# Pacing side work beside a first attention: scans given twice their share of a chain's order of work, and weight preparation that ends 2.4 batches in

## The chip, the cores and the metric

The kernel runs on one core of one Trainium2 chip. A core has a matrix engine (TensorE, PE in the profile; PEld is its weight load), a vector engine (VectorE, DVE), a scalar engine (ScalarE, ACT), a general engine (GpSimd, POOL) and SyncE (SP), which here issues all DMA transfers. The metric is device time in microseconds (us) of one execution; lower is better.

## The reference, cut to what matters

Eight batches of 64 rows of 512 values pass through six layers. The first is a large cross attention of 32 heads on a context of 1601 rows for each batch; the others are small by comparison.

```python
def reference(x, ctx_4096, ...):          # x (8, 64, 512), ctx_4096 (8, 1601, 512)
    x = x + xattn0(layernorm(x), ctx_4096)  # 32 heads of 128, 8 key/value heads, softmax, Wo
    x = x + mamba(layernorm(x))             # state space layer, below
    x = x + ternary_ffn(layernorm(x))       # 512 x 512 ternary weights, one scale
    x = x + xattn1(layernorm(x), ctx_4096)  # one head, softmax(x ctx^T) ctx, no weights
    x = x + attn1(layernorm(x))             # 32 heads of 16, rotary, causal
    x = x + oct_ffn(layernorm(x))           # gate, up, down; ternary, octonion structure
    return x

def mamba(h):                              # 1024 channels, 16 states
    x, gate = split(h @ W_in.T)
    x = silu(conv4(x) + conv_b)
    ts, Bm, Cm = rms each of split(x @ W_x.T)
    dt = softplus(ts @ W_dt.T + b_dt)
    for t in range(64):                    # the scan, for every channel and state
        state = state * exp(dt[t] * A) + dt[t] * x[t] * Bm[t]
        y[t] = sum over states of state * Cm[t]
    return ((y + x * D) * silu(gate)) @ W_out.T
```

Weights of the small layers are split into two float32r parts or made ternary before use. That preparation is part of the kernel: it reads the weights from HBM, works on them and writes the results to a scratch buffer in HBM.

## The kernel before, in words

**Main stream.** `x_all` is the first attention. It goes through 64 units, one for each batch and key/value head, 8 units to a batch. In each it projects keys (`x_k`, line 363) and values (`x_v`, line 334), multiplies scores (`x_s`, line 385), finds a row maximum (`mx`, lines 390 to 395), and one unit later takes exponentials (`x_exp`, lines 426 and 427), sums them on POOL (line 452) and multiplies by the values (`x_av`, line 464). After two batches it multiplies by Wo (`x_wo`, line 521) and adds into the tile `x1` (line 524). VectorE stands inside this loop: the copies of keys (`kt`, line 109), maxima and exponentials' inputs must be done before PE's next step can run, and the PSUM tag `kv` of those steps has 4 buffers.

**Side work.** Two kinds of generators run beside it. `prep` (lines 607 and on) prepares the weights: 100 steps of 1.5 to 3 units of cost, each of a load, one to three operations on ACT, DVE and POOL, and a store. In order these write `d_wout`, `d_ffn`, `d_wat`, `d_gu`, `d_dn` and `d_wo`. `chain` carries two batches through the five small layers. There are four chains, 0 to 3; one starts when its two batches have left the first attention. Chains 0 to 2 run beside the attention of later batches. Chain 3 starts when the attention has ended, in a different form (`tail`), with pools made anew in the memory that the attention and the first layers' tiles leave (`xctx.close()`, `actx.close()`).

**Order of work.** The order is written out by a small planner in `run`. Each yield of `x_all` gives a cost; their running sum divided by `X_COST = 236` is the position `now` in batches. A side generator has a total `cost`, a start and an end, and after each step of the main stream it is advanced until what it has yielded equals `cost * (now - start) / (end - start)`. So a yield's number is the share of the generator's window that the code before it gets. A chain's cost is `CHAIN_COST = 377`, and the lengths of its windows are `SPAN = [3.1, 3.1, 2.6, 0.2]` batches. Preparation has `PREP_COST = 168` and ends at `PREP_END = 2.8`. In units of cost, a side chain (0 to 2) yields, in order:

- `mamba`: convolution and its input 24, state inputs 3, `dt` 16, scans 128 (32 scans of 4 yields of 1, line 907 and on), gates and output 14.4
- `ternary_ffn` 9, `xattn1` 76 (38 for each batch), `attn1` 44, `oct_ffn` 33

The sum is 347.4, so a chain has yielded all before its window's end. When the attention ends, `now` goes on in steps of 0.01 with chain 3 first in the list and what is left of chain 2 behind it.

**Queues.** The Tile framework turns this program order into instruction queues by scheduling against a model of the machine, earlier work first. Side work on DVE, ACT and POOL is pinned: an instruction stays behind whatever was traced just before it on its engine (`Late`, line 65, which is why all of it stands under L65 in the profile). Instructions of the main stream are not pinned and may move ahead. PE and SP are not pinned. All chains and the preparation share 2 PSUM buffers of tag `acc`; the scans use none of them, but the `ca` pool's tags, `a2` with 5 buffers among them.

**One scan** (lines 893 to 916) is 4 of the 16 states of 128 channels: four exponentials on ACT, a memset and one or two products on POOL, yield, the scan on DVE, yield, a product with C on DVE or POOL in turn, yield, a reduction and an addition on DVE, yield. For each group of 8 scans two DMAs spread B and C over the partitions (line 889).

Of the kernel before, what the change touches and what calls it, by code (L numbers as in the profile page):

```python
# [78 lines left out]
class Kernel:  # L79
# [727 lines left out]
    def mamba(self, gi, x, xo):  # L807
# [87 lines left out]
        def scan(c, sh, bc):  # L895
            da = self.sb(self.td, [P, HS, 2, T])
            for s in range(HS):
                k = sh * HS + s
                nc.scalar.activation(da[:, s], dt[:, c], AF.Exp, scale=self.A[:, c, k : k + 1])
            nc.gpsimd.memset(da[:, :, :, 0:1], 0.0)  # L900
            du = dus[:, c]
            if sh == 0:
                nc.gpsimd.tensor_tensor(du, dt[:, c], u[:, c], ALU.mult)
            h = self.sb(self.ts, [P, HS, 2, T])
            nc.gpsimd.tensor_tensor(h, bc[:, 0], du[:, None].to_broadcast([P, HS, 2, T]), ALU.mult)

            yield 1
            hf, df = h.rearrange("p s b t -> p (s b t)"), da.rearrange("p s b t -> p (s b t)")
            nc.vector.tensor_tensor_scan(hf, df, hf, 0.0, ALU.mult, ALU.add)
            yield 1  # L910
            (nc.gpsimd if c % 2 else nc.vector).tensor_tensor(h, h, bc[:, 1], ALU.mult)
            yield 1
            y = da[:, 0]
            nc.vector.tensor_reduce(y.rearrange("p b t -> p (b t)"), h.rearrange("p s b t -> p (b t) s"), AX.X, ALU.add)
            nc.vector.scalar_tensor_tensor(u[:, c], u[:, c], self.Dp[:, c : c + 1] if sh == 0 else 1.0, y, ALU.mult, ALU.add)
            yield 1

        wps = None
        if tail:
# [43 lines left out]
        else:  # L963
            for sh in range(nh):
                bc = bcast(sh)
                for c in range(NCH):
                    yield from scan(c, sh, bc)
# [332 lines left out]
    def run(self):  # L1300
        nc, tc, ctx = self.nc, self.tc, self.ctx
        nc.scalar.preload_act_table_set("natural_log_exp_and_others")
        self.setup(bufs=BUFS, accb=2, hs=4, tail=False, ahead=1, **TAGS)
        self.pc = ctx.enter_context(tc.tile_pool(name="pc", bufs=2, space=PSUM))
        xctx = ctx.enter_context(ExitStack())
        self.px = xctx.enter_context(tc.tile_pool(name="px", bufs=2, space=PSUM))
        self.consts()
        self.scratch()
        self.xw = ctx.enter_context(tc.tile_pool(name="xw", bufs=2))
        self.xp = xctx.enter_context(tc.tile_pool(name="xp", bufs=2))  # L1310
        qctx = ctx.enter_context(ExitStack())
        self.q_ln(qctx.enter_context(tc.tile_pool(name="qp", bufs=2, side="right")))
        B = self.B
        sizes = GROUPS.get(B) or [1] * B
        groups, k = [], 0
        for m in sizes:
            groups.append(list(range(k, k + m)))
            k += m
        self.place = {b: (k * T, len(g) * T) for g in groups for k, b in enumerate(g)}
        side, self.tp = [], None  # L1320

        def start(gen, now, cost, end):
            env = {k: getattr(self, k) for k in ENV}
            if not self.tail:
                env["nc"] = Side(self, PINNED)
            side.append({"gen": gen, "cost": cost, "got": 0.0, "t0": now, "end": end, "env": env})

        def advance(now):
            base = {k: getattr(self, k, None) for k in ENV}
            for c in list(side):  # L1330
                self.setup(**c["env"])
                goal = c["cost"] * min(1.0, (now - c["t0"]) / max(c["end"] - c["t0"], 1e-9))
                if now >= c["end"]:
                    goal = 1e9
                while c["got"] < goal:
                    try:
                        c["got"] += next(c["gen"])
                    except StopIteration:
                        if PRINT_COST:
                            print("side", c["got"])  # L1340
                        side.remove(c)
                        break
            self.setup(**base)

        gi, now, xdone = 0, 0.0, 0.0
        for cost, fin in self.x_all(list(range(B))):
            xdone += cost
            if not self.flush:
                advance(xdone / X_COST)
            if fin == 0:  # L1350
                qctx.close()
                self.cp = ctx.enter_context(tc.tile_pool(name="cp", bufs=2, side="right"))
                actx = ctx.enter_context(ExitStack())
                self.ca = actx.enter_context(tc.tile_pool(name="ca", bufs=2, side="right"))
                start(self.prep(), xdone / X_COST, PREP_COST, PREP_END)
            if fin is not None and gi < len(groups) and groups[gi][-1] == fin:
                g = groups[gi]
                now = xdone / X_COST
                last = gi == len(groups) - 1
                if last:  # L1360
                    self.pinning = False
                    xctx.close()
                    actx.close()
                    self.pc = ctx.enter_context(tc.tile_pool(name="pt", bufs=3, space=PSUM))
                    self.ca = self.cp = self.tp = ctx.enter_context(tc.tile_pool(name="tp", bufs=2))
                    self.setup(bufs=BUFS_TAIL, accb=6, hs=8, tail=True, ahead=2, **TAGS_TAIL)
                start(self.chain(gi, g), now, CHAIN_COST, now + SPAN[gi])
                if last:
                    side.insert(0, side.pop())
                gi += 1  # L1370
        while side:
            now += 0.01
            advance(now)
# [4 lines left out]
ENV = ("nc", "cp", "ca", "pc", "bufs", "accb", "hs", "tail", "ahead", *TAGS)  # L1378
GROUPS = {8: [2, 2, 2, 2], 2: [2]}
SPAN = [3.1,3.1,2.6,0.2]  # L1380
PREP_END = 2.8
MAMBA_TAGS = ("a2", "lv", "bc", "xpad", "sm")
FFN_TAIL = (("l", 0), ("l", 1), ("a", 0), ("l", 2), ("a", 1), ("d", 0), ("a", 2), ("d", 1), ("d", 2))
REST = {"w2":8,"b4":3}
# [3 lines left out]
PREP_COST = 168.0  # L1388
PRINT_COST = False
CHAIN_COST = 377.0  # L1390


@with_exitstack
# [106 lines left out]
```

## Time and profile before

| | |
|---|---|
| runs | 2731.54 us median of 3 (2730.45 to 2734.26) |
| profiled execution: span, first to last instruction | 2719.3 us |
| its own time | not listed apart from its span; the median lies 12.2 us above the span |
| mean granted clock of TensorE | 0.977 |
| busy: PE, PEld, DVE, ACT, POOL | 94%, 84%, 64%, 50%, 43% |
| DMA | 455.59 MB, 52.2% of 16 engines' span |
| DVE scans of chains 0, 1, 2 (first to last start) | 769 to 1041, 1411 to 1691, 2033 to 2308 us |
| `mamba` ends in chains 0, 1, 2 (its `xr` starts being written) | 1124.2, 1784.6, 2387.8 us |
| last store of prepared weights is issued | 879.7 us |
| the attention's last result (`x1`, line 524) starts | 2423.2 us |
| chain 2's last result, chain 3's last result (line 1294) | 2702.3, 2715.6 us |

A busy share is the sum over stages that have different limits. In a table of stretches of time, each engine's busy time stands beside the length of the stretch, and PEclk is the share of full clock that the throttle granted TensorE there. Idle time of PE matters as long as PE is what the stretch is short of.

### The profile page before, as it was taken

The numbers are of one execution on the slowest core, as the hardware profiler recorded it, in microseconds if no ns is written. First come the engines' busy times: TensorE is split into PE (matmuls) and PEld (weight loads), VectorE is DVE, ScalarE is ACT, GpSimd is POOL, SyncE is SP. The second block draws the span as 40 slices with busy tenths as digits, with TensorE's granted clock in tenths as the row PEclk, the third lists the DMA queues.
The fourth block names the chain that finished last, engine by engine and source line by source line (L and its number), as shares of the span: only waits on it lengthen the run. The fifth ranks groups of instructions, "written<-read, shape, count | busy, mean of one in ns | idle before, by whom it ended". The sixth has DMA issues, their size and how long they took to land.

```text
span 2719.3 us, 43920 instructions
## 1 busy us (share of the span) xinstructions
PE 2565.7 (94%) x16288; PEld 2273.7 (84%) x16288; DVE 1746.8 (64%) x2843; ACT 1352.6 (50%) x3128; POOL 1171.4 (43%) x1123
## 2 busy tenths in 40 slices
PE   7999999999998899999999988999999998986888
PEld 6999999889887899978988987997897898964644
DVE  4544345577688886545568689544668879457854
ACT  4444554445565554544455554544555455445543
POOL 3212434464588643422357346421249445114610
PEclk9999999999999999999999998999999999997999
DMA  9544446665665234665234443565342463476575
GB/s 308 153 141 153 138 144 228 200 204 178 214 218 188 75 121 159 211 184 174 88 109 134 152 136 106 185 206 186 116 133 80 128 187 113 148 256 201 195 264 188
DMA packets 302934, 455.59 MB, mean 168 GB/s; under 512 B 80248, under 2 KB 179576, under 8 KB 298240
## 3 DMA queue, kind: packets, MB, share of 16 engines
q1 hardware_dynamic: 302720, 452.79, 52.2%
q8 instruction: 128, 2.10, 0.3%
q14 instruction: 86, 0.70, 0.1%
HBM read 380.23 MB, written 72.48 MB: 166 GB/s over the span
## 4 chain that ended last, share of the span: by engine, by line
PE 47%; DVE 11%; DMA 4%; POOL 3%; issue 3%; ACT 2%; POOLq 0%; DVEq 0%; ACTq 0%; SPq 0%
PE v_ps L334 10%; PE k_ps L363 10%; PE o_ps L464 6%; PE s_ps L385 5%; DVE a L65 4%; PE w_ps L521 2%; PE acc L819 2%; PE acc L777 2%; PE acc L774 1%; PE acc L1092 1%; PE acc L1036 1%; POOL a L65 1%; POOL ss L452 1%; DVE acc L953 1%; PE acc L1178 1%
## 5 line engine op out<-in xcount | busy, mean ns | idle before, releaser
L363 PE MATMUL k_ps<-cxb,wk 128*128 128x384 f32 x2304 | 473.5, 348 | 36.4 <-DVE kt L109 12.6
L334 PE MATMUL v_ps<-wv,cxb 128*128 128x256 f32 x3456 | 474.1, 283 | 7.4 <-DVE mx L392 3.9
L334 PEld LDWEIGHTS v_ps<-wv,cxb 128*128 128x128 f32 x3456 | 441.8, 190 | 28.9 <-issue 13.6
L363 PEld LDWEIGHTS k_ps<-cxb,wk 128*128 128x128 f32 x2304 | 406.8, 192 | 56.3 <-DVE kt L109 14.3
L385 PE MATMUL s_ps<-q,kt 128*128 128x256 f32 (+1 forms) x2496 | 414.5, 299 | 8.6 <-DVE mx L392 7.2
L464 PE MATMUL o_ps<-S,v 128*128 128x256 f32 (+1 forms) x1664 | 413.6, 381 | 2.6 <-DVE rw L479 1.7
L388 ACT COPY S<-s_ps 128x512 f32<-128x512 f32 (+1 forms) x448 | 242.5, 554 | 252.6 <-PE s_ps L385 249.0
L385 PEld LDWEIGHTS s_ps<-q,kt 128*128 128x128 f32 (+1 forms) x2496 | 342.0, 185 | 30.3 <-DVE mx L392 8.5
L392 DVE TENSOR_TENSOR mx<-s_ps,mx 128x512 f32<-128x512 f32 x256 | 175.4, 685 | 297.5 <-ACT S L388 297.2
L452 POOL TENSOR_TENSOR ss<-ss,S 128x512 f32<-128x512 f32 x254 | 356.6, 1404 | 14.9 <-ACT S L427 0.3
L429 POOL TENSOR_TENSOR ss<-S,S 128x512 f32<-128x512 f32 x64 | 84.0, 1312 | 640.0 <-ACT S L427 639.9
L464 PEld LDWEIGHTS o_ps<-S,v 128*128 128x128 f32 (+1 forms) x1664 | 299.4, 190 | 41.6 <-issue 5.6
L426 DVE TENSOR_TENSOR S<-S,m_ps 128x512 f32<-128x512 f32 (+1 forms) x448 | 257.5, 641 | 36.2 <-PE m_ps L412 35.4
L108 ACT ACTIVATE kt<-k_ps,c_bk 128x384 fp32r<-128x384 f32 (+1 forms) x256 | 151.8, 593 | 246.2 <-PE k_ps L363 245.4
L427 ACT ACTIVATE S<-S 128x512 f32<-128x512 f32 (+1 forms) x448 | 247.6, 600 | 41.4 <-DVE S L426 41.0
L109 DVE SCALAR_TENSOR_TENSOR kt<-k_ps,c_bk,kt 128x384 fp32r<-128x384 f32 (+1 forms) x256 | 160.9, 629 | 156.2 <-ACT kt L108 155.0
L337 ACT COPY v<-v_ps 128x256 f32<-128x256 f32 (+1 forms) x416 | 152.1, 368 | 195.8 <-PE v_ps L334 192.7
L334 PE MATMUL v_ps<-wv,cxt 128*128 128x256 f32 (+1 forms) x1536 | 211.3, 286 | 5.1 <-DVE mx L392 5.1
L334 PEld LDWEIGHTS v_ps<-wv,cxt 128*128 128x128 f32 (+1 forms) x1536 | 194.6, 176 | 17.3 <-issue 5.9
L363 PE MATMUL k_ps<-cxt,wk 128*128 128x450 f32 x768 | 179.3, 376 | 0.0
L65 DVE TENSOR_TENSOR_SCAN a<-a,a 128x512 f32<-128x512 f32 x96 | 153.9, 1603 | 32.2 <-POOL a L65 32.0
L65 ACT ACTIVATE a<-lv,c_A_log 128x128 f32<-128x128 f32 x384 | 122.8, 392 | 85.8 <-DVE a L65 84.8
(358 smaller groups left out, 3951.3 us busy)
## 6 DMA issues: line engine op xcount, KB each, us to landing
wo<-d_wo SPq DMA_DIRECT2D x96, 512.0 KB, 5.6
wk<-d_wk SPq DMA_DIRECT2D x63, 512.0 KB, 4.3
wv<-d_wv SPq DMA_DIRECT2D x31, 1024.0 KB, 5.7
cst<-in_ctxT_dram SPq DMA_DIRECT2D x96, 192.0 KB, 2.7
b<-in_ctxN_dram SPq DMA_DIRECT2D x36, 512.0 KB, 3.8
d_q<-q_t SPq DMA_DIRECT2D x32, 512.0 KB, 4.3
q<-d_q SPq DMA_DIRECT2D x64, 256.0 KB, 3.0
d_wo<-b SPq DMA_DIRECT2D x32, 512.0 KB, 2.9
```

The lines of the kernel that those rows point to most:

```text
L65: return lambda *a, **k: self.tc.keep_in_program_order(f(*a, **k))
L109: eng.scalar_tensor_tensor(lo, src, bias, hi.bitcast(FP), ALU.add, ALU.subtract)
L334: nc.tensor.matmul(ps[:r], lhsT=cx[:, a, c, o : o + r], rhs=w[:, m, c, :], start=k == 0, stop=k == 11)
L337: nc.scalar.copy(vt[:r], ps[:r])
L363: nc.tensor.matmul(ps[:, :wd], lhsT=w[:, a, c, :], rhs=cx[:, m, c, :], start=k == 0, stop=k == 11)
L385: nc.tensor.matmul(sp[:r, gi, :], lhsT=kt[:, a, o : o + r], rhs=q[:, m, :], start=k == 0, stop=k == 2)
L388: nc.scalar.copy(s[:r, :n], sp[:r, :n])
L392: nc.vector.tensor_tensor(mx, sp, S[0] if len(S) == 1 else mx, ALU.max)
L426: nc.vector.tensor_tensor(sv, sv, ps[:r, 1:2].to_broadcast([r, w, 256]), ALU.add)
L427: nc.scalar.activation(sv, sv, AF.Exp, scale=ISC)
L452: nc.gpsimd.tensor_tensor(ss, ss, S[n], ALU.add)
L464: nc.tensor.matmul(ps[:, 0], lhsT=self.v[(b, j, t)][:r, hc : hc + P], rhs=S[t // 2][:r, t % 2], start=t == 0, stop=t == NT - 1)
```

## The change

The four yields of a side chain's scan become 2 in place of 1, so that a chain's scans yield 256 units and not 128. The planner is told: a chain that is not the last has a cost of 377 + 128 = 505. Windows (`SPAN`) stay. So the scans get 256 of 505 parts of a window where they had 128 of 377, and every other step of a chain is spread over 377/505 = 0.747 of the positions that it had. The last chain is untouched. Preparation of weights, whose steps and cost stay, ends at 2.4 batches. No instruction is added or removed; what changes is the order in which the program is written, and what the scheduler makes of it.

```diff
--- before.py
+++ after.py
@@ -904,16 +904,16 @@
             h = self.sb(self.ts, [P, HS, 2, T])
             nc.gpsimd.tensor_tensor(h, bc[:, 0], du[:, None].to_broadcast([P, HS, 2, T]), ALU.mult)
 
-            yield 1
+            yield 2
             hf, df = h.rearrange("p s b t -> p (s b t)"), da.rearrange("p s b t -> p (s b t)")
             nc.vector.tensor_tensor_scan(hf, df, hf, 0.0, ALU.mult, ALU.add)
-            yield 1
+            yield 2
             (nc.gpsimd if c % 2 else nc.vector).tensor_tensor(h, h, bc[:, 1], ALU.mult)
-            yield 1
+            yield 2
             y = da[:, 0]
             nc.vector.tensor_reduce(y.rearrange("p b t -> p (b t)"), h.rearrange("p s b t -> p (b t) s"), AX.X, ALU.add)
             nc.vector.scalar_tensor_tensor(u[:, c], u[:, c], self.Dp[:, c : c + 1] if sh == 0 else 1.0, y, ALU.mult, ALU.add)
-            yield 1
+            yield 2
 
         wps = None
         if tail:
@@ -1364,7 +1364,7 @@
                     self.pc = ctx.enter_context(tc.tile_pool(name="pt", bufs=3, space=PSUM))
                     self.ca = self.cp = self.tp = ctx.enter_context(tc.tile_pool(name="tp", bufs=2))
                     self.setup(bufs=BUFS_TAIL, accb=6, hs=8, tail=True, ahead=2, **TAGS_TAIL)
-                start(self.chain(gi, g), now, CHAIN_COST, now + SPAN[gi])
+                start(self.chain(gi, g), now, CHAIN_COST if last else CHAIN_COST + SCAN_MORE, now + SPAN[gi])
                 if last:
                     side.insert(0, side.pop())
                 gi += 1
...
 SPAN = [3.1,3.1,2.6,0.2]
-PREP_END = 2.8
+PREP_END = 2.4
...
 CHAIN_COST = 377.0
+SCAN_MORE = 128.0
```

## The prediction

> **What bounds the kernel now.** I read the engines' shares first, then a table of stretches, then the groups of VectorE in the scans' stretches, the waits of PE there, and last the starts of each layer's last write.
>
> ```profile
> PE 2565.7 (94%) x16288; PEld 2273.7 (84%) x16288; DVE 1746.8 (64%) x2843; ACT 1352.6 (50%) x3128; POOL 1171.4 (43%) x1123
> ...
> PE   7999999999998899999999988999999998986888
> ...
> DVE  4544345577688886545568689544668879457854
> ```
>
> PE is nearly always busy and dips where DVE's digits reach 7 to 8: while scans run, and in the tail from 2412 us on. Stretches (us; then busy time of PE, PEld, DVE, ACT, POOL; granted clock; DMA share; GB/s):
>
> ```profile
> 640.00:768.00 128.00, 124.52 (x821) 115.95 (x820) 93.87 (x160) 70.41 (x160) 68.46 (x65) 0.97 0.62 201
> 768.00:855.00 87.00, 73.48 (x454) 69.37 (x453) 77.60 (x82) 48.45 (x116) 75.27 (x70) 0.92 0.66 218
> 855.00:1045.00 190.00, 180.09 (x1189) 171.63 (x1187) 157.51 (x218) 106.26 (x262) 118.27 (x114) 0.99 0.37 112
> 1045.00:1300.00 255.00, 254.85 (x1675) 222.02 (x1675) 131.30 (x246) 118.47 (x271) 70.14 (x68) 1.00 0.57 183
> 1411.00:1600.00 189.00, 185.37 (x1244) 170.94 (x1243) 144.72 (x214) 104.93 (x249) 110.27 (x107) 1.00 0.44 136
> 1600.00:1695.00 95.00, 78.41 (x453) 71.71 (x452) 85.71 (x112) 45.37 (x122) 49.22 (x52) 0.89 0.33 106
> 2033.00:2222.00 189.00, 180.32 (x1168) 160.87 (x1167) 154.59 (x217) 102.56 (x253) 120.57 (x118) 0.99 0.39 116
> 2222.00:2310.00 88.00, 80.78 (x503) 74.46 (x502) 75.83 (x111) 46.72 (x119) 48.52 (x48) 0.98 0.47 145
> 2412.00:2719.00 307.00, 241.20 (x1338) 154.24 (x1337) 193.04 (x366) 141.09 (x372) 89.55 (x96) 0.88 0.67 224
> ```
>
> Without scans (1045 to 1300) PE has no gap. With scans and `prep` together (768 to 855) it idles 13.5 of 87 us. Chain 1 shows what density does, by the scans' group on DVE from 1411 to 1600 and from 1600 to 1695:
>
> ```profile
> L65 DVE TENSOR_TENSOR_SCAN a<-a,a 128x512 f32<-128x512 f32 x15 | 24.0, 1601 | 3.3 <-POOL a L65 3.2
> L65 DVE TENSOR_TENSOR_SCAN a<-a,a 128x512 f32<-128x512 f32 x18 | 27.6, 1536 | 6.7 <-POOL a L65 6.7
> ```
>
> One scan in 12.6 us cost PE 3.6 us in 189; one in 5.3 us cost 16.6 us in 95. There PE waits for the main stream's own DVE work, queued behind scans:
>
> ```profile
> PE k_ps L363 <- DVE mx L392: 4.7, 1, 4.7
> PE s_ps L385 <- DVE mx L392: 4.5, 1, 4.5
> ```
>
> **Where the change puts things.** I turn planned positions into times by the unit then running in this trace (the transposes on line 412 open each). Scans of chains 0, 1, 2 are planned for 764 to 1054, 1346 to 1677, 1951 to 2224 us and began at 769, 1411, 2033. Their new plan is 735 to 1178, 1322 to 1795, 1922 to 2333: one in 13.8, 14.8 and 12.8 us, against 9.1, 10.3 and 8.5. Preparation's plan ends at 745, not 868 (its last store is issued at 880). The end of chain 2's `mamba` moves from 2252 to 2355.
>
> **Scans spread.** A scan step issues four exponentials on ACT (0.39 us each), a memset and products on POOL (1.3 to 1.4 us), the scan (1.54 to 2.47), a product on DVE or POOL (1.0 or 1.3), a reduction (1.06) and an addition (0.5): 3.6 us of DVE on average. All remains; 8 scans still share two DMAs through SP. What can go is PE's loss. Idle time while scans run is 13.5 + 9.9 = 23.4 us (chain 0), 3.6 + 16.6 = 20.2 (chain 1), 8.7 + 7.2 = 15.9 (chain 2). Lost clock is at most (1 - granted) x length: 8.9, 10.5 and 3.7 more. At the sparse rate, 3.6/15 = 0.24 us, 32 scans cost 7.7 us. So chain 0 gains 15.7 to 24.6; I take 19, between them, since POOL's preparation leaves as well. Chain 1 gains 12.5 to 23.0, nothing if the bunch only moves; I take 12.5, idle alone, since it starts late. Chain 2: if scans begin at 2033 again, 300 us are left to 2333, one in 9.4 us, which is nearest to 2033 to 2222 (189/19 = 9.9 us, 8.7/19 = 0.46 us each): 32 cost 14.7, a gain of 1; bounds are a loss of 6 (more of them bunched) and a gain of 11.9. Sum: 32.5.
>
> **Preparation earlier.** The same steps, with 2 DMAs each for the split ones, pass ACT, DVE, POOL and SP in 367 planned us rather than 490. What they cost PE without scans is 4.4 us idle from 378 to 640, 3.5 from 640 to 768 and 3.8 of clock: 11.7. In proportion to work nothing changes; with the square of density it grows by a third. I take +4, bounds 0 and +12. Main-stream transfers that share SP with its 32 stores of `d_wo` meet them some 120 us earlier; the first `wo` read that needs them belongs to batch 3, past 900, so no one waits for the result. What covered the late stores, the scans of chain 0, loses them.
>
> The scans' own time shows that neighbour: 2472 ns each from 768 to 855 beside `prep` on POOL, 1606 from 855 on. The Trainium skill, SBUF — State Buffer, section Who interferes with whom, states that a VectorE instruction with two SBUF inputs and a GpSimd instruction reading SBUF shut each other out for a whole instruction. That speaks against spreading: a sparse scan meets the attention's own POOL sums instead, and by 1601 against 1536 ns 96 scans would pay 6 us more of DVE time. No term here holds those 6 us.
>
> **The rest of a chain, denser.** 1045 to 1300 shows `mamba`'s output, `ternary_ffn` and `xattn1` with 0.15 us of PE idle and DVE at 51%. Packed into 0.747 of the positions, their DVE above the attention's own (44% from 120 to 378) rises by some 3 points, far from the 82% of 2033 to 2222. A stretch like 640 to 768 (2.7% idle) over the 341 + 353 planned us of chains 0 and 1 would cost 19. I take +3, bounds 0 and +19. Scans of the next chain now lie beside all of `attn1` and `oct_ffn`; the `dt` step no longer does. Today its second half waits for an `acc` buffer from 1307.8 to 1383.0 (line 872) behind `attn1`'s projections, 18 us each by weight loads (line 774).
>
> **The tail.** These DVE lines end chain 2's `mamba`, chain 2 and chain 3:
>
> ```profile
> 2387.77 0.69 DVE L65 TENSOR_TENSOR xr<-acc,x 128x512 f32<-128x512 f32 x1 [1.20 <-PE acc L777]
> ...
> 2702.34 0.75 DVE L1294 SCALAR_TENSOR_TENSOR xr<-acc,s_oct,xr 128x512 f32<-128x512 f32 x1
> ...
> 2715.59 0.75 DVE L1294 SCALAR_TENSOR_TENSOR xr<-acc,s_oct,xr 128x512 f32<-128x512 f32 x1 [2.92 <-PE acc L777]
> ```
>
> `mamba` ended 36, 78 and 136 us behind its plan in chains 0, 1, 2. From 2355 that is 2391 to 2491; I take 2415, between the first two since `dt` meets less, just before the attention's last sum at 2423. Chain 3 is then not held. Chain 2's rest took 2702.3 - 2387.8 = 314.5 us; from 2415 it ends at 2729.5, past today's 2719.3: +10. Bounds: +67 if `mamba` ends at 2491 and chain 3's memory waits for it; -16 if chain 3's 128 projections on line 819 (35 us for 19.1 of PE) run alone since chain 2 comes later.
>
> **Sum.** -32.5 + 4 + 3 + 10 = -15.5: span 2703.8. The median stands 12.2 above the span; with that unchanged, 2716.0 us.
>
> **Rivals.** Slower by the tail: chain 2's `mamba` ends after 2423 and holds chain 3 one for one. For it: the lateness grew along the chains. Against it: bunched scans cannot delay it once few are overdue, and the engines are free after 2412. It decides from 2423 + 25.5 = 2449 on; at 2465 it gives -25.5 + 42 = +16.5, 2748. Slower by density: chain 1 gains nothing, preparation costs 12 and the rest 19: -19 - 1 + 12 + 19 + 10 = +21, 2753. For it: PE idles 3.5 us from 640 to 768, where a chain's start meets `prep`. Against it: 1045 to 1300. No change: what sets the scans' pace is lateness, not the order (chains 1 and 2 began 65 and 82 us late), so only chain 0 beside `prep` gains 9 (13.5 to the 5% of 855 to 1045), against 4 + 3: about 2730.
>
> **How the numbers follow.** Likeliest 0.54, own range 2692 to 2726; tail 0.22; density 0.10; no change 0.14. A measurement tells 0.2%, 5.5 us, from no change. The best ends of all terms give -75, the worst +88, and need all terms at once; 2688 leaves out one in ten below, 2760 one above. Faster 0.54, same 0.14, slower 0.32.
>
> **What would show it.** Right: scans near 740 to 1180, 1400 to 1800 and 2030 to 2330 without a bunch like 1600 to 1695; no `d_wo` store after about 770; PE idle near 8 us in each of the first two chains' scans; chain 2's `mamba` ended before the attention's last sum, and its last result at the end of the trace. Wrong: scans still bunched at the end, or chain 3's first layer norm waiting for chain 2.

## The result, and the profile after

The changed kernel takes 2742.32 us (median of 9 runs, 2736.41 to 2747.24). Beside it the kernel before took 2731.54 us (9 runs, 2724.19 to 2735.69). The ratio is 1.0043, 95% interval 1.003 to 1.0055: slower by 0.3 to 0.55%. The prediction said 2716.0 us and faster. The time lies within the whole range that it gave, 2688 to 2760, but outside the 2692 to 2726 of its likeliest case, and the sign is wrong. The nearest forecast is that of its rival "slower by the tail", 2748.

A warning on the traces. In the profiled executions the span went from 2719.3 to 2741.3 us, 22.0 us more, but the medians are only 10.8 us apart. All later profiled executions took 1.7 to 2.5 us more than their span, so the profiled execution of before took about 2721 us, some 10 us below its median. The trace of preparation alone (first experiment) is a better base: it is the first step of the change, and its execution took 2733.22 us against a median of 2733.31. Two more profiled executions were short, that of {2} by 5.1 us and that of the kernel with a window of 2.3 by 7.1; the rest lie within 2.2 us of their medians.

The engines' shares and slices of the changed kernel:

```profile
PE 2570.2 (94%) x16288; PEld 2280.3 (83%) x16288; DVE 1703.3 (62%) x2843; ACT 1353.1 (49%) x3128; POOL 1174.0 (43%) x1123
...
PE   7999999999998999999999998899999999757887
...
DVE  4544345766768766656656658756576657848754
...
PEclk9999999999999999999999999999999999877998
```

The dip of PE in slice 13 stays, but the next slice is full. The dip of chain 1 is still there (slices 25 and 26), and a new one opens in slices 35 to 37, just where the attention ends.

Stretches of the changed kernel (us, length, busy PE, PEld, DVE, ACT, POOL, granted clock, DMA share, GB/s). The first row holds 25 of chain 0's 32 scans (the other 7 start by 1125, and PE has no idle time from 1045 to 1130), the second the work after them; then come chain 1's scans before and after chain 0's last result; then chain 2's scans before and after chain 1's last result; then the wait for chain 2, and the tail:

```profile
814.00:1045.00 231.00, 222.37 (x1467) 211.78 (x1466) 175.56 (x257) 127.39 (x310) 139.80 (x133) 0.99 0.34 102
1130.00:1354.00 224.00, 224.00 (x1519) 199.75 (x1518) 129.17 (x244) 109.54 (x253) 64.64 (x63) 1.00 0.48 152
1354.00:1650.00 296.00, 295.22 (x1912) 264.24 (x1911) 179.90 (x304) 149.74 (x347) 129.99 (x126) 1.00 0.47 148
1650.00:1762.00 112.00, 89.96 (x530) 82.73 (x529) 103.66 (x132) 61.31 (x160) 82.71 (x79) 0.91 0.44 131
1984.00:2306.00 322.00, 319.95 (x2065) 286.51 (x2064) 207.07 (x344) 167.43 (x388) 143.05 (x140) 1.00 0.46 147
2306.00:2378.00 72.00, 51.53 (x299) 46.14 (x297) 65.27 (x84) 31.71 (x90) 44.59 (x46) 0.84 0.20 63
2378.00:2438.00 60.00, 36.09 (x140) 25.70 (x140) 19.45 (x41) 12.81 (x33) 4.35 (x8) 0.76 0.44 140
2438.00:2741.00 303.00, 236.48 (x1332) 155.53 (x1332) 193.08 (x374) 140.21 (x374) 91.00 (x93) 0.86 0.69 229
```

Chain 0's scans now cost PE 8.6 us in 231. Chains 1 and 2 do as before, only more sharply: PE idles 0.8 us in 296 and then 22.0 in 112; 2.0 in 322 and then 20.5 in 72. DVE is busy 93% and 91% of the time in those two bunches. In them the scans' group on DVE reads (chain 1, then chain 2):

```profile
L65 DVE TENSOR_TENSOR_SCAN a<-a,a 128x512 f32<-128x512 f32 x18 | 31.4, 1746 | 3.6 <-POOL a L65 3.6
L65 DVE TENSOR_TENSOR_SCAN a<-a,a 128x512 f32<-128x512 f32 x14 | 22.6, 1618 | 5.0 <-POOL a L65 5.0
```

So 18 and 14 of the 32 scans run after the older chain's last result, one every 6.1 and 5.0 us. Doubling their share did not remove the bunches. In the kernel before it was 16 and 10, behind last results at 1608.9 and, 57.1 us earlier than now, at 2249.1:

```profile
2249.11 0.74 DVE L65 SCALAR_TENSOR_TENSOR xr<-acc,s_oct,xr 128x512 f32<-128x512 f32 x1
```

The end of the attention in the changed kernel, by VectorE's instructions in order of time (start, us, line, operation, tiles):

```profile
2306.19 0.73 DVE L65 SCALAR_TENSOR_TENSOR xr<-acc,s_oct,xr 128x512 f32<-128x512 f32 x1
...
2405.67 0.69 DVE L524 TENSOR_TENSOR x<-w_ps,x 128x512 f32<-128x512 f32 x1 [3.59 <-PE w_ps L521]
...
2437.49 0.69 DVE L65 TENSOR_TENSOR xr<-acc,x 128x512 f32<-128x512 f32 x1 [11.11 <-PE acc L777]
2438.10 0.68 DVE L141 BATCH_NORM_STATS2 ln_st<-x 128x6 f32<-128x512 f32 x1
...
2732.09 0.75 DVE L1294 SCALAR_TENSOR_TENSOR xr<-acc,s_oct,xr 128x512 f32<-128x512 f32 x1 [0.97 <-PE acc L777]
...
2737.22 0.75 DVE L1294 SCALAR_TENSOR_TENSOR xr<-acc,s_oct,xr 128x512 f32<-128x512 f32 x1 [2.92 <-PE acc L777]
```

These are, in order: chain 1's last result, the attention's last sum, the end of chain 2's `mamba`, chain 3's first layer norm, and the last results of chains 2 and 3. The attention ends 17.5 us earlier than before (2423.2), but chain 2's `mamba` ends 49.7 later (2387.8), and chain 3 starts directly behind it, 32.4 us after the attention's last sum. In the kernel before it started 1.2 us behind that sum:

```profile
2423.17 0.67 DVE L524 TENSOR_TENSOR x<-w_ps,x 128x512 f32<-128x512 f32 x1
...
2424.36 0.68 DVE L141 BATCH_NORM_STATS2 ln_st<-x 128x6 f32<-128x512 f32 x1
```

In every run of this study in which that `mamba` ended after the attention, chain 3 started 0.6 us behind it; in every run in which it ended before, chain 3 started 0.7 to 1.2 us behind the attention. The hold is shown. That its cause is the memory chain 3 shares with the first layers' tiles is read from the code and was not tried: chain 3's first layer norm also stands directly behind that `mamba`'s last instruction on VectorE, so the order of VectorE's own queue would show the same.

I split the span at chain 3's first layer norm: 2424.4 + 294.9 before, 2438.1 + 303.2 after. Below, "start" is the first part and "tail" the second. Against preparation alone, the better base (2424.2 + 307.2), the start is 13.9 us longer and the tail 4.0 shorter: the loss is the hold.

How much of the attention's 17.5 us was real? From 120 us to its end, first before, then after:

```profile
120.00:2423.00 2303.00, 2229.68 (x14415) 2033.00 (x14413) 1501.16 (x2403) 1159.04 (x2662) 1052.34 (x994) 0.99 0.50 157
```

```profile
120.00:2406.00 2286.00, 2214.66 (x14310) 2023.86 (x14308) 1449.01 (x2376) 1153.37 (x2643) 1053.01 (x993) 0.98 0.49 155
```

PE's idle time is 73.3 us before and 71.3 after. Of the 17 us, 2.0 are idle time saved and 15.0 are PE work: 105 matmuls, nearly all of chain 2, that used to run beside the attention and now run behind it.

### The profile page after: what moved, and what is told of

It reads as the page before. It is cut to its first block, busy times and chain, and to the rows that moved or that the text cites. A ratio compares the mean times of both kernels' runs of the same rounds, so it can differ in the third digit from the quotient of the medians.

```text
span 2741.3 us, 44008 instructions
## 1 busy us (share of the span) xinstructions
PE 2570.2 (94%) x16288; PEld 2280.3 (83%) x16288; DVE 1703.3 (62%) x2843; ACT 1353.1 (49%) x3128; POOL 1174.0 (43%) x1123
## 4 chain that ended last, share of the span: by engine, by line
PE 33%; DVE 9%; DMA 4%; POOL 2%; ACT 1%; issue 1%; SPq 0%; DVEq 0%; POOLq 0%
PE v_ps L334 6%; PE k_ps L363 6%; PE o_ps L464 4%; DVE a L65 4%; PE s_ps L385 3%; PE acc L774 2%; PE acc L777 2%; PE w_ps L521 1%; PE acc L819 1%; PE acc L1036 1%; PE acc L1178 1%; PE acc L1092 1%; POOL a L65 1%; PE acc L776 1%; DMA a<-in_W_inT_dram 1%
## 5 line engine op out<-in xcount | busy, mean ns | idle before, releaser
L363 PE MATMUL k_ps<-cxb,wk 128*128 128x384 f32 x2304 | 474.7, 348 | 29.0 <-DVE mx L392 11.7
L452 POOL TENSOR_TENSOR ss<-ss,S 128x512 f32<-128x512 f32 x254 | 354.6, 1396 | 15.7 <-ACT S L427 0.3
L65 DVE TENSOR_TENSOR_SCAN a<-a,a 128x512 f32<-128x512 f32 x96 | 147.4, 1536 | 30.4 <-POOL a L65 28.3
```

The lines of the kernel that those rows point to most:

```text
L65: return lambda *a, **k: self.tc.keep_in_program_order(f(*a, **k))
L363: nc.tensor.matmul(ps[:, :wd], lhsT=w[:, a, c, :], rhs=cx[:, m, c, :], start=k == 0, stop=k == 11)
L452: nc.gpsimd.tensor_tensor(ss, ss, S[n], ALU.add)
```

## The experiments

Each table column is read from the trace of that kernel: the end of the attention (its last sum starts), the end of chain 2's `mamba`, chain 3's start and the tail. "Left" is how many scans of chains 1 and 2 start after the older chain's last result. Ratios are against the kernel before on the same chip, with 95% intervals. Chains in braces are those with the doubled share.

| kernel | attention ends | `mamba` 2 ends | start + tail | left, 1 / 2 | median | ratio |
|---|---|---|---|---|---|---|
| before | 2423.2 | 2387.8 | 2424.4 + 294.9 | 16 / 10 | 2731.54 | 1 |
| preparation to 2.4 alone | 2423.0 | 2387.6 | 2424.2 + 307.2 | 16 / 10 | 2733.31 | 1.0026 [1.0016, 1.0036] |
| {0} | 2400.2 | 2404.8 | 2405.4 + 316.6 | 13 / 10 | 2724.75 | 0.9997 [0.9983, 1.001] |
| {1} | 2398.6 | 2399.9 | 2400.5 + 315.1 | 19 / 8 | 2717.28 | 0.9954 [0.9937, 0.9971] |
| {2} | 2424.8 | 2397.3 | 2425.5 + 293.7 | 16 / 16 | 2726.34 | 1.0003 [0.9992, 1.0014] |
| {0, 1} | 2398.0 | 2398.6 | 2399.2 + 313.8 | 18 / 8 | 2714.80 | 0.9960 [0.9945, 0.9975] |
| {0, 2} | 2397.3 | 2406.8 | 2407.4 + 301.1 | 13 / 16 | 2712.43 | 0.9945 [0.993, 0.9959] |
| {1, 2} | 2404.2 | 2419.3 | 2419.9 + 309.4 | 19 / 14 | 2729.78 | 0.9998 [0.9985, 1.0011] |
| {0, 1, 2}: the change | 2405.7 | 2437.5 | 2438.1 + 303.2 | 18 / 14 | 2742.32 | 1.0043 [1.003, 1.0055] |

All rows from the second on have preparation end at 2.4.

### The two halves of the change

Preparation alone, in the kernel before:

```diff
-PREP_END = 2.8
+PREP_END = 2.4
```

> Preparation ends at 2.4, scans keep their old share. Theory 'held tail' (the changed kernel is slower because chain 2's mamba ends after the attention and holds chain 3): this edit leaves chain 2's plan alone, so its mamba ends near 2388 us and before the attention's last sum, and only the gain of scans without preparation beside them is left: 2715 to 2727 us. Rival 'density' (denser side steps cost the attention PE time): preparation is denser by a third, 2733 to 2742 us.

Measured: 2733.31 us beside 2726.92, ratio 1.0026. The attention ended at 2423.0, 0.2 us from before, and its stretch shows the same idle time (74.4 us against 73.3):

```profile
120.00:2423.00 2303.00, 2228.64 (x14412) 2029.13 (x14410) 1481.91 (x2404) 1155.14 (x2662) 1053.98 (x995) 0.99 0.50 157
```

So inside the attention the move costs nothing and gains nothing. The held tail's 2715 to 2727 was missed. The 2733 to 2742 that the density theory expected was hit, but not by its mechanism. The 12 us that this trace has more than that of before all lie behind the attention, with the same 1284 matmuls there (the row of before is 2424 to 2719: 232.01 of 295.00 busy, clock 0.88):

```profile
2424.00:2731.00 307.00, 236.84 (x1284) 153.16 (x1284) 188.79 (x356) 138.00 (x366) 87.55 (x92) 0.84 0.64 215
```

They arise late, in chain 3 alone. Chain 2's last result starts at 2702.2 us (2702.3 before), chain 3's at 2727.7 (2715.6). The rows from 2424 to 2600 are alike (PE 132.2 us before, 131.2 here); those from 2640 to 2700, first before, then here, are not:

```profile
2640.00:2700.00 60.00, 53.00 (x266) 31.97 (x264) 28.01 (x51) 24.84 (x49) 8.27 (x9) 1.00 0.76 261
2640.00:2700.00 60.00, 47.24 (x220) 25.24 (x220) 25.58 (x50) 20.46 (x42) 7.99 (x9) 0.93 0.75 254
```

Some 10 us of it may be that the profiled execution of before was shorter than its median. Why the end of chain 3 differs stays open.

The scans alone (the changed kernel with the old end of preparation):

```diff
-PREP_END = 2.4
+PREP_END = 2.8
```

> Scans get twice their share in chains 0 to 2, preparation ends at 2.8 as before. Held tail: chain 2's mamba ends again some 10 to 20 us after the attention's last sum, and the scans of chain 0 meet preparation again: 2740 to 2756 us. Density: without the denser preparation part of the loss is gone, 2731 to 2738 us.

Measured: 2754.50 us, ratio 1.0103 [1.0085, 1.012]. The attention ended at 2403.6, `mamba` 2 at 2435.1, the tail took 316.0. As the held tail expected, the scans cause the hold (31.5 us here, 10 to 20 expected), not the preparation. Beside these scans the earlier preparation is a gain: by the ratios the changed kernel, which has both, is 0.6% faster.

### Which chain's scans

The yields and the cost are doubled for some chains only:

```diff
-            yield 2
+            yield 2 if gi in SCAN_TWICE else 1
...
-                start(self.chain(gi, g), now, CHAIN_COST if last else CHAIN_COST + SCAN_MORE, now + SPAN[gi])
+                start(self.chain(gi, g), now, CHAIN_COST + (SCAN_MORE if gi in SCAN_TWICE else 0), now + SPAN[gi])
...
+SCAN_TWICE = (0, 1)
```

> The change as it is, but chain 2 keeps its old share and cost (yields of 1, 377). Held tail: chain 2's scans are ahead in the order again, its mamba ends by 2425 us, chain 3 is held by less than 5 us: 2718 to 2732 us. Density: chains 0 and 1 are as dense as in the changed kernel, 2736 to 2745 us.

Measured: 2714.80 us, ratio 0.996 [0.9945, 0.9975], faster than both kernels; by the ratios some 23 us under the changed one, and 28.3 us by the spans. The direction is that of the held tail; the time is below its range.

```profile
2398.03 0.69 DVE L524 TENSOR_TENSOR x<-w_ps,x 128x512 f32<-128x512 f32 x1 [8.90 <-PE w_ps L521]
2398.64 0.68 DVE L65 TENSOR_TENSOR xr<-acc,x 128x512 f32<-128x512 f32 x1
2399.24 0.68 DVE L141 BATCH_NORM_STATS2 ln_st<-x 128x6 f32<-128x512 f32 x1
```

Chain 2's `mamba` now ends as the attention does, and chain 3 starts 38.9 us earlier than in the changed kernel. The tail gives back 10.6.

With `SCAN_TWICE = (0,)`:

> Only chain 0's scans get twice their share; preparation ends at 2.4. Held tail: the gain in chain 0's scans (PE idle 23.4 to about 9 us) stays, chain 2's mamba ends before the attention's last sum: 2710 to 2724 us. Density: one chain of three is still denser, 2730 to 2738 us.

Measured: 2724.75 us, just above its range, and `mamba` 2 ended 4.6 us behind the attention, not ahead of it; ratio 0.9997. Against preparation alone the attention ends 22.8 us earlier: PE's idle time from 120 us to its end falls from 74.4 to 61.0, and 9.7 us of work move behind it.

```profile
120.00:2400.00 2280.00, 2218.99 (x14360) 2026.89 (x14358) 1469.83 (x2385) 1154.30 (x2654) 1054.63 (x993) 0.99 0.50 157
```

The tail is 9.4 us longer and chain 3 starts 5.2 us behind the attention rather than 1.2, so only 9.4 us of span, 8.6 of the median, remain of the 22.8.

With `SCAN_TWICE = (2,)`:

> Only chain 2's scans get twice their share (its cost is 505); chains 0 and 1 are as before; preparation ends at 2.4 as in the changed kernel. Theory (chain 2 is late because chain 1 already was, and its own stretch comes on top): chain 2 starts at its old 1839, its `mamba` takes the 576 us that it took in the changed kernel rather than 549 and ends near 2415, ahead of the attention's last sum at 2423 to 2431; chain 3 is not held, its first layer norm follows that sum by less than 5 us; span 2727 to 2738, median 2728 to 2740. Rival (chain 2's doubling has a price by itself, whatever the older chains do): the 28 us of span between the changed kernel and the one with chains 0 and 1 alone come on top of the 2731 of preparation alone; `mamba` ends past 2440, chain 3 starts there, median 2752 to 2765.

Measured: 2726.34 us, ratio 1.0003. `mamba` 2 ended at 2397.3, 9.7 us later than without and still ahead of the attention. Chain 2's doubled scans cost nothing by themselves (2733.31 with preparation alone). The rival is out, and the time is a little below the theory's range. On top of chains 0 and 1 the same edit costs 28.3 us of span (2713.0 to 2741.3). The prices of the chains don't add.

### What makes chain 2 late: windows

A longer window for chain 2 in the kernel before, to put its `mamba` behind the attention without touching the scans:

```diff
-SPAN = [3.1,3.1,2.6,0.2]
+SPAN = [3.1,3.1,3.1,0.2]
```

> The kernel before with chain 2's window 3.1 batches long in place of 2.6, nothing else: its mamba is planned to end some 85 us later and no scan gets another share. Held tail: mamba ends at 2440 to 2470 us, chain 3's first layer norm follows it at once and not the attention's last sum: 2745 to 2775 us. Rival 'length of the tail' (what counts is how much of chain 2 is left, and chain 3 is not held): chain 3 starts within 5 us of the attention's last sum, at most 2740 us.

Measured: 2737.77 us, ratio 1.0045 [1.0029, 1.0061]. The `mamba` ended 41.6 us later, at 2429.3, but the attention also ended later, at 2432.0 (PE idled 23.6 us in chain 2's scans, 15.9 before), so nothing was held. The held tail's 2745 to 2775 is missed, and the experiment missed its aim of making a hold: the attention beside the larger bunch became later too. The rival's forecast (no hold, at most 2740) was met, but its reason, a longer tail, does not show: the tail was 302.3 us, 307.2 with preparation alone.

A shorter window for chain 2 in the changed kernel:

```diff
-SPAN = [3.1,3.1,2.6,0.2]
+SPAN = [3.1,3.1,2.2,0.2]
```

> The changed kernel with chain 2's window 2.2 batches long in place of 2.6: its scans keep twice their share, but its mamba is planned to end 0.25 batches (some 75 us) earlier. Held tail: mamba ends at 2395 to 2420 us, chain 3 starts with the attention's last sum, 2715 to 2730 us. If chain 2's scans are held back by chain 1's layers and not by their plan, mamba still ends after 2425 us: 2735 to 2745 us.

Measured: 2779.57 us, ratio 1.0195 [1.0165, 1.0226]. Both times expected were missed. The `mamba` ended only 5.6 us earlier, at 2431.9, and the tail grew to 344.2 us. The last results of chains 2 and 3:

```profile
2738.09 0.75 DVE L1294 SCALAR_TENSOR_TENSOR xr<-acc,s_oct,xr 128x512 f32<-128x512 f32 x1 [0.34 <-PE acc L777]
...
2772.57 0.75 DVE L1294 SCALAR_TENSOR_TENSOR xr<-acc,s_oct,xr 128x512 f32<-128x512 f32 x1 [2.59 <-PE acc L777]
```

They are 34.5 us apart, 5.1 in the changed kernel. By the constants the short window writes chain 2's rest ahead of chain 3's last layers; chain 3 ends alone.

The same with chains {0, 1} and a window of 2.3:

```diff
-SPAN = [3.1,3.1,2.6,0.2]
+SPAN = [3.1,3.1,2.3,0.2]
...
+SCAN_TWICE = (0, 1)
```

> Twice the share in chains 0 and 1 alone, preparation to 2.4, and chain 2's window 2.3 batches long in place of 2.6, so that its mamba is planned some 40 us earlier and less of chain 2 is left for the tail. If chain 2's lateness at the attention's end is what remains of the loss: mamba ends some 20 to 40 us ahead of the attention's last sum, the tail falls from 314 to 300 us, 2700 to 2712 us. If chain 2 is bound by chain 1's layers: 2712 to 2722 us.

Measured: 2756.29 us, ratio 1.0108 [1.0084, 1.0133]; both expectations were missed. `mamba` 2 ended later (2409.7), not earlier, behind a last result of chain 1 at 2325.2 rather than 2284.9, and the tail was 337.1.

And the other way, chains {0, 1} with a window of 2.8:

```diff
-SPAN = [3.1,3.1,2.6,0.2]
+SPAN = [3.1,3.1,2.8,0.2]
```

> The kernel in which chains 0 and 1 alone have the doubled share, with chain 2's window 2.8 batches long rather than 2.6. Theory (the tail is long where chain 2's rest stands ahead of chain 3's last layers in the order): chain 2's `mamba` ends some 17 us later, near 2415, and chain 3, held, starts there; but chain 2's rest moves behind chain 3's layers, so the tail is 303 to 308 us and not 313.8; median 2716 to 2726. Rival (only the hold counts, the tail does not change): start near 2415 and a tail of 313 to 318, median 2728 to 2736. Third case (the `mamba` is not later, the tail is shorter all the same): median 2702 to 2712.

Measured: 2715.60 us, ratio 0.9958 [0.9945, 0.9971]. Chain 3 started at 2409.5, 10.3 us later, and the tail was 303.0, 10.8 us shorter. The median is 0.4 us under the theory's range; rival and third case are out. With 337, 314 and 303 us at 2.3, 2.6 and 2.8 batches, the tail does depend on where chain 2's rest stands in the order, and here hold and tail cancel.

This holds beyond these three. In every held kernel the tail starts at the same point of chain 2's work. By how far behind the attention the constants plan chain 2's end (its share of the window, less 2 batches), the tails are 344.2 us at 0.07 batches, 337.1 at 0.12, 313.8 to 316.6 at 0.40 ({0}, {1}, {0, 1}), 301.1 to 309.4 at 0.45 (four kernels with chain 2 doubled) and 303.0 at 0.58. Only the scans alone, with preparation to 2.8, fall out: 316.0 at 0.45.

Last, chain 1's window in the changed kernel:

```diff
-SPAN = [3.1,3.1,2.6,0.2]
+SPAN = [3.1,2.8,2.6,0.2]
```

> The changed kernel with chain 1's window 2.8 batches long rather than 3.1. Theory (chain 2 is late because chain 1 already was): chain 1's `ternary_ffn`, behind which chain 2's first layer norm stood until 1861, and its `oct_ffn`, behind which the bunch of scans stood until 2306, both end some 25 to 35 us earlier; chain 2's `mamba` ends near 2412 rather than 2437, chain 3 starts there, with a tail of 303 to 315: median 2714 to 2730. Rival (the stretch of chain 2's own scans decides, not chain 1's lateness): chain 2 begins earlier, but its `mamba` still ends at 2430 to 2440; median 2734 to 2750.

Measured: 2750.75 us, ratio 1.0085 [1.007, 1.0099]. My theory fell; the rival came nearer (its 2430 to 2440 and 2734 to 2750 are just passed). Chain 1's last result came 27 us earlier (2279.3) and chain 2's first layer norm came 18.5 us earlier (1842.9), as it said, but `mamba` 2 ended 9 us later, at 2446.6, and the attention ended at 2398.7, so chain 3 was held 48 us. The scans' group behind chain 1's last result, and the stretch:

```profile
L65 DVE TENSOR_TENSOR_SCAN a<-a,a 128x512 f32<-128x512 f32 x21 | 32.0, 1525 | 6.3 <-POOL a L65 6.3
```

```profile
2279.00:2394.00 115.00, 80.66 (x437) 70.61 (x436) 106.21 (x141) 52.68 (x143) 65.68 (x67) 0.84 0.26 80
```

There are now 21 scans behind it and not 14: 7 more at 5.4 us are 38 us, more than the 27 gained. This is what the lateness theory lacked: how many scans the written order leaves behind the older chain.

With `SCAN_TWICE = (0, 2)`:

> Chains 0 and 2 have the doubled share, chain 1 is as before; preparation ends at 2.4. Theory A (work that any older chain hands on is enough: with chain 0 alone doubled, chain 2's `mamba` ended at 2404.8, 4.6 us behind the attention, and a stretched chain 2 comes on top): `mamba` ends 2425 to 2440, chain 3 is held 20 us or more, median 2728 to 2746. Theory B (it takes chain 1's lateness): chain 2 begins by 1830, its `mamba` ends by 2412, chain 3 starts at 2400 to 2412; median 2712 to 2728.

Measured: 2712.43 us, ratio 0.9945 [0.993, 0.9959], the lowest of the study, though its interval overlaps those of {1} and {0, 1}. Theory B's numbers: chain 2 began at 1823.7, `mamba` 2 ended at 2406.8, chain 3 started at 2407.4.

```profile
2397.26 0.69 DVE L524 TENSOR_TENSOR x<-w_ps,x 128x512 f32<-128x512 f32 x1 [3.05 <-PE w_ps L521]
...
2406.81 0.69 DVE L65 TENSOR_TENSOR xr<-acc,x 128x512 f32<-128x512 f32 x1 [8.86 <-PE acc L777]
2407.42 0.69 DVE L141 BATCH_NORM_STATS2 ln_st<-x 128x6 f32<-128x512 f32 x1
```

### The pins

The scans of the changed kernel, not pinned behind what was traced before them:

```diff
+            self.pinning = False
...
+            self.pinning = True
             yield 2
...
```

> The changed kernel with the scans' own instructions not pinned behind the instruction traced before them. If pinning behind the older chain's layers makes the scans late and then bunched: scans of chain 1 follow their plan (one in 12 to 16 us from about 1350 to 1790 us, no gap over 40 us), PE idles under 12 us in them in place of 20.9, and chain 2's mamba ends by 2420 us: 2710 to 2730 us. If lateness has another cause (buffers, weights' loads), gaps of 60 us and the bunch stay: 2735 to 2750 us.

Measured: 2781.13 us, ratio 1.0193 [1.0166, 1.0221], far above both times expected. The bunches behind the older chain are gone: each chain's 32 scans run 6.1 to 6.4 us apart without a gap over 12 us, from 807, 1391 and 2024 us, ahead of the older chain's last result. But that is the bunch's own pace, now for all 32, and PE idles 29.4, 28.5 and 24.9 us in the three stretches:

```profile
807.00:997.00 190.00, 160.56 (x989) 149.20 (x987) 177.84 (x222) 105.87 (x277) 141.44 (x136) 0.94 0.29 87
1391.00:1590.00 199.00, 170.46 (x1035) 142.85 (x1033) 185.32 (x246) 109.43 (x288) 140.60 (x137) 0.95 0.35 106
2024.00:2221.00 197.00, 172.07 (x995) 142.69 (x994) 186.79 (x241) 107.16 (x283) 141.28 (x137) 0.92 0.33 106
```

The attention ended at 2479.7. So it is the pins that hold scans behind the older chain; and without them nothing paces the scans at all.

### A count worked out from the constants

After twelve runs this account fitted: a side instruction stays behind what was traced before it, so the scans that are *written* behind the older chain's last result also *run* behind it. How many these are follows from the constants: the older chain has yielded all of its 347.4 (475.4 if doubled) at that share of its window, and the younger one has then had that position, less 2 batches, over its window, times its cost; 43 units go to the steps ahead of its scans, the rest to scans at 4 units each (8 if doubled). Before the change this leaves 16.7 scans of chain 1 and 11.7 of chain 2; after it 18.7 and 15.1. Measured were 16, 10, 18 and 14, and in all the pinned kernels the count was within 3 of the arithmetic, mostly 0 to 2 below it. Of chain 2, `mamba` ended at the older chain's last result, plus 4.1 to 5.9 us for each scan left, plus 53 to 83 us. The two last runs were forecast by it. With `SCAN_TWICE = (1,)`:

> Only chain 1's scans get twice their share; preparation ends at 2.4. Account by the order: side work is pinned, so the scans that are written behind the older chain's last result wait for it and then run at 5.0 to 6.1 us each, and `mamba` ends 60 to 95 us behind the last. Worked out from the constants: chain 0 has yielded all at 347.4/377 x 3.1 = 2.857 batches, 0.857 behind chain 1's start; chain 1 has yielded 0.857/3.1 x 505 = 139.6 by then, 43 of them ahead of the scans, so 96.6/8 = 12.1 scans are done and 19.9 left (16.7 before the change). For chain 2: chain 1 ends at 475.4/505 x 3.1 = 2.918, and 0.918/2.6 x 377 = 133.1 leaves 9.5. Forecast: 18 to 20 of chain 1's scans start behind chain 0's end (near 1610), its `mamba` ends 1785 to 1815 and no PE time is won there (idle 17 or more); 8 to 10 of chain 2's scans are left, its `mamba` ends 2365 to 2405; the attention ends at 2415 to 2427, chain 3 follows it; median 2718 to 2734. Rival (a doubled share spreads the scans): at most 14 left, idle at most 12, `mamba` of chain 1 by 1785, the attention ends 8 to 12 us before 2423.

Measured: 2717.28 us, ratio 0.9954 [0.9937, 0.9971], just below the forecast. The counts are 19 and 8, as forecast, and `mamba` 2 ended at 2399.9, in its range. But for chain 1 the times were not: chain 0 had ended by 1584.7, the 19 scans took 8.9 us each and not 5 to 6, `mamba` 1 ended at 1832.8 (forecast 1785 to 1815), and PE idled 13.0 us there, not 17 or more. The attention ended at 2398.6, 24.4 us earlier than with preparation alone, where neither the account nor its rival had it. The row of chain 1's scans:

```profile
1371.00:1760.00 389.00, 376.04 (x2451) 348.13 (x2451) 279.82 (x419) 206.87 (x491) 213.22 (x206) 0.99 0.42 133
```

So the count behind the older chain says which scans come late, but not that they bunch. Behind a chain 0 that is not doubled, chain 1's 19 scans took 8.9 us each, here and in the next run, with 13.0 and 11.8 us of PE idle time; behind a doubled one, 18 took 6.1 each with 20.6 to 20.9 ({0, 1} and the changed kernel). That they bunch when they are overdue, and were not here because chain 0 ended early (1584.7, 1650.7 in {0, 1}), is argued and was not tried.

With `SCAN_TWICE = (1, 2)`:

> Chains 1 and 2 have the doubled share, chain 0 is as before; preparation ends at 2.4. Account by the order: chain 1 as with its own doubling alone (18 to 20 scans left, `mamba` ends 1785 to 1815); of chain 2, 0.918/2.6 x 505 = 178.3, less 43, is 16.9 scans done, 15.1 left; 14 or 15 start behind chain 1's end, which lies between 2255 and 2300, so the `mamba` ends at that time + 14.5 x 5.2 + 64, 2394 to 2440; without chain 0's gain the attention ends at 2415 to 2430 and chain 3 is held 10 us or less; median 2718 to 2742. Rival (the price of the three together is that of chains 1 and 2 together): chain 2's `mamba` ends 25 us or more behind the attention as in the changed kernel; median 2745 to 2765.

Measured: 2729.78 us, ratio 0.9998 [0.9985, 1.0011], in the forecast; the rival's 2745 to 2765 is out. 14 scans of chain 2 were left, `mamba` 2 ended at 2419.3 (forecast 2394 to 2440). The attention ended at 2404.2, earlier than forecast, so chain 3 started 15.7 us behind it, more than the 10 expected and half of the changed kernel's 32.4.

## Why the prediction was wrong, step by step

**The step that failed: the tail.** The prediction took 2415 for the end of chain 2's `mamba`, "just before the attention's last sum at 2423. Chain 3 is then not held". It ended at 2437.5, while the attention ended at 2405.7. The rival "slower by the tail" was the right mechanism, and its objection, that "bunched scans cannot delay it once few are overdue", was the error: 14 were left, not few. The 50 us of lateness add up so, most of them handed on by chain 1: its last result came 57.1 us later (2249.1 to 2306.2), the scans left took 69.3 us and not 58.9 (14 and 10), and the end of the `mamba` behind the last scan was 17.7 us shorter: 57.1 + 10.4 - 17.7 = 49.8. The prediction also set 2415 against the old end of the attention, though its own terms moved that end to about 2398 (2423 - 25.5; measured 2405.7). Unless chain 2 moved along, which it did not say and which did not happen, 2415 was a hold of some 17 us already. The term of +10 was +13.7 in the start, even though the attention ended 17.5 earlier, and +8.3 in the tail: 22.0 against the short trace of before; against preparation alone it is +13.9 and -4.0. Chain 2's rest, taken as 314.5 us, was 294.6.

The likeliest case could have been tested with the constants that it quoted. It turned planned positions into times, but counted no scans against the older chain's end, and left out that each doubled chain's planned end itself moves, from 2.857 to 2.918 batches, some 18 us. Measured, chain 0's last result moved by 41.1 (1608.9 to 1650.0) and chain 1's by 57.1.

**Scans spread, -32.5.** Chain 0, -19: right in its place, somewhat high in size. Idle time in its scans fell from 23.4 before to 8.6 in the changed kernel ("near 8"): 14.8, just under the lower bound of 15.7, and 3.6 of them came from preparation's move. When it alone was doubled, it fell from 19.8 to 8.5, and the attention ended 22.8 us earlier. But 9.7 of these are work moved behind the attention, and of the span 9.4 remained. The steps did not price moved work at all. Chain 1, -12.5: on top of chain 0 it moved the attention's end by 2.2 us, and the idle time in its scans rose from 12.5 to 20.6. The lower bound, "nothing if the bunch only moves", was the value. Alone, chain 1 would have given 24.4 us; the gains exclude one another. It isn't the count that tells the two apart: 19 scans were left in {1} and 18 in {0, 1}, but chain 0's last result came at 1584.7 and 1650.7, and only the 18 bunched. Chain 2, -1: on top of the other two, idle time rose from 10.4 to 20.4 us and the attention ended 7.7 us later, near the loss of 6 that was the bound; the hold is charged above.

**Preparation earlier, +4.** Nothing in the attention (0.2 us earlier), but a median 6.4 us up, which lies behind it and whose cause is open. Its last store is issued at 813 us in the changed kernel and not before 770, so the planned 745 ran 68 us late.

**The rest of a chain, +3.** At its lower bound of 0 where chain 0's rest runs alone: from 1130 to 1354 PE has no idle time at all.

**From span to time.** "The median stands 12.2 above the span; with that unchanged" was wrong: it stands 1.0 above it now. The offset was one short execution, not a property of the kernel. It would have made the prediction 10 us lower, not nearer.

**"No change"** said that lateness and not the order sets the pace, and that only chain 0 gains. Half of that holds, for chains 1 and 2 with all three doubled; {0, 2} and {1} show that the order can win some 0.5%.

**The neighbour.** The trace agrees with what the prediction cited from the Trainium skill, SBUF — State Buffer, Who interferes with whom (a VectorE instruction with two SBUF inputs and a GpSimd instruction that reads SBUF exclude one another). With preparation done before 815 us, chain 0's 32 scans in the first experiment read

```profile
L65 DVE TENSOR_TENSOR_SCAN a<-a,a 128x512 f32<-128x512 f32 x32 | 51.2, 1600 | 10.0 <-POOL a L65 10.0
```

where 10 of them beside `prep` had taken 2472 ns each. The feared price of sparse scans, 6 us, came out the other way. In the changed kernel the bunched scans took 1746 and 1618 ns each, and the sparse ones ahead of them (chain 1, 1354 to 1650, then chain 2, 1984 to 2306)

```profile
L65 DVE TENSOR_TENSOR_SCAN a<-a,a 128x512 f32<-128x512 f32 x14 | 17.9, 1282 | 3.9 <-POOL a L65 2.0 <-ACT a L65 2.0
L65 DVE TENSOR_TENSOR_SCAN a<-a,a 128x512 f32<-128x512 f32 x18 | 24.1, 1338 | 2.1 <-POOL a L65 2.1
```

In the stretches of the two kernels a scan's time goes, roughly, with the share in which POOL is busy: 1282 and 1338 ns at 44%, 1366 to 1618 at 52 to 62%, 1672 at 64%, 1746 at 74%, 2472 at 87%. The share alone does not set it: in the unpinned kernel a scan took 1605 to 1733 ns at 71 to 74%. DVE's busy time fell from 1746.8 to 1703.3 us with the same 2843 instructions, and the kernel still became slower: a smaller sum of DVE work did not help while the work that PE waited for stood in bunches.

**What stays open:** the 12 us at the end of the first experiment's chain 3, why chain 0 ends earlier in {1} and {1, 2} (1584.7 and 1585.7) than with preparation alone (1610.2), and whether memory or the order of VectorE's queue makes chain 3 wait.

## What to carry to other kernels

When side work is kept in written order behind older side work, a step made sparse makes its own chain end later, and the next chain inherits that. Work out from the planner's constants when each older chain ends and how much stands behind that end before asking how sparse the step is: making it sparse in every chain moved the last results of chains 0 and 1 by 41 and 57 us and put chain 2's `mamba` behind the attention, while doing it in every second chain (0 and 2) won 0.55%. An earlier end of the bounding stage is a gain only as far as its idle time fell; compare idle time and busy time up to that end (here 2.0 and 15.0 us), and look at who holds the next stage. Take a single profiled execution's distance from the median for scatter until a second trace shows otherwise.

## What was not expected of the hardware

While chain 3 was held, PE had 14.24 us of work in 32 and its granted clock fell to 0.72; over the whole bunch and hold, from 2305 to 2438, it was 0.80:

```profile
2406.00:2438.00 32.00, 14.24 (x52) 8.30 (x52) 4.97 (x11) 3.85 (x11) 0.21 (x4) 0.72 0.43 138
2305.00:2438.00 133.00, 88.62 (x444) 72.79 (x442) 85.72 (x127) 45.40 (x124) 49.86 (x54) 0.80 0.31 99
```

So a hold costs the work inside it speed as well: a matmul of line 777 (128x512) took 0.39 us at 2407 and 0.63 at 2427. And scatter differs between orders of the same work: on one chip 21 runs of the kernel before lie between 2720.5 and 2734.5 us, and the five of {0, 1} between 2714.6 and 2716.0.
